# A recommendation kernel on one core: GpSimd takes a product of each of the first two chunks, VectorE reads factors from PSUM

## The chip, the cores and the metric

The kernel runs on one core of one Trainium2 chip. The metric is the device time in microseconds. Before the change it is 501.09 us, the median of three runs (500.9 to 501.11).

Five engines work side by side and meet only at semaphores: TensorE (PE, matmuls out of SBUF into PSUM), VectorE (DVE), ScalarE (ACT), GpSimd (POOL), and SyncE (SP), which here issues nearly all DMAs.

## The reference

A three-layer compressed interaction network for 1024 rows of 64 fields with 16 elements each, everything in float32. Cut to what matters:

```python
x0 = x; h = x; xs = []                                   # x: (1024, 64, 16)
for i in range(3):
    z = jnp.einsum('bfe,bge->bfge', x0, h).reshape(B, 64 * fh, 16)
    y = jnp.einsum('oc,bce->boe', Ws[i], z) + bs[i][None, :, None]   # 128 outputs
    if i != 2:
        x_i, h = y[:, :64], y[:, 64:]                     # half is pooled, half goes on
    else:
        x_i, h = y, y
    xs.append(x_i)
pooled = jnp.sum(jnp.concatenate(xs, axis=1), axis=2)
return pooled @ fc_w.T + fc_b                             # (1024, 1)
```

What is needed is the products of pairs of fields of x (z of the first layer), contracted with weights. As the result is summed and then weighted by `fc_w`, the kernel folds the later layers' weights together beforehand, and contracts the same z with them.

## The kernel before

The 1024 rows are cut into 32 chunks of 32 rows, so that a chunk has N = 512 columns (32 rows by 16 elements). For each chunk two tiles of x are loaded, `xa` (128 partitions, 4 blocks i of 512) and `xb` (4 blocks j of 512). One product per j makes a z tile of 128 x 4 x 512: block i of `xa` times block j of `xb`, so every i meets every j. TensorE then contracts the 16 blocks with the 16 blocks of `w_all`.

```python
HEAD = [4, 5, 6, 0, 1]            # the chunks c0, c1, c2, c3, c4 of the head
NI = NJ = 4

def product(c, j, pieces=1):
    zs[c, j] = z_tile(f"z_{c}_{j}")
    n = NI // pieces
    for i in range(0, NI, n):
        nc.vector.tensor_tensor(
            zs[c, j][:, i : i + n, :], xas[c][:, i : i + n, :],
            xbs[c][j].unsqueeze(1).to_broadcast([128, n, N]), ALU.mult,
        )
    if j == NJ - 1:
        nc.scalar.activation(zs[c, j][SQ, 0, :], xas[c][SQ, 0, :], AF.Square)
```

The head comes first: five chunks are contracted with the first layer's weights only, 64 columns of `w_all` (part 0), while the folded weights (the second 64 columns) are still being made. The first layer's weights of a pair (f, g) and (g, f) are summed on VectorE, one sum for each j; both halves lie in the SBUF tile `w0t`.

```python
def h1_weights(j):
    nc.vector.tensor_tensor(
        w_all[:, j * NI : (j + 1) * NI, 0:64], w0s[j][:, :, 0, :], w0s[j][:, :, 1, :], ALU.add
    )

def half_contract(c, part, j):     # group j of chunk c: 4 blocks, 2 halves of the columns
    cols = slice(part * F, (part + 1) * F)
    rows = slice(0, F) if part == 0 and j == NJ else slice(0, 128)
    for t in (NT,) if j == NJ else range(j * NI, (j + 1) * NI):
        z = zls[c] if t == NT else zs[c, j][:, t % NI, :]
        for n in range(2):
            nc.tensor.matmul(
                accs[c][halves[n]], w_all[rows, t, cols], z[rows, n * H2 : (n + 1) * H2],
                start=(t == 0), stop=(t == NT),
            )
```

In the profile each of these float32 matmuls is two records, so a group is 16 records. `squares(c)` makes the last, smaller tile (`zl`) on ScalarE, and `keep_h1(c)` evacuates a chunk's sums.

The loads in the order of their issue on SyncE (cut to names): first half of xa of c0, block 0 of xb of c0 (`in_xh`), second half of xa of c0, block 0 of w0t (`in_wh`), blocks 1 to 3 of xb of c0, blocks 1 to 3 of w0t, xa and xb of c1, the two 1 MB tiles `w2s`, xa and xb of c2, and `w1s` (1 MB). Then the head of the work:

```python
new_acc(c0, H2)
squares(c0)
for j in range(NJ):
    product(c0, j, 2 if j == 0 else 1)
    if j == NJ - 1:
        nc.vector.memset(w0s[j][SQ, 0, 1, :], 0.0)
    h1_weights(j)
nc.vector.tensor_copy(w_all[0:32, NT, 0:64], w0ds[0:32])
for j in range(NJ + 1):
    half_contract(c0, 0, j)
keep_h1(c0)
squares(c1)
load_chunk(c3)

for n in range(2):                 # sums over w2s with fc weights: pv, evacuated to v2r
    ...
new_acc(c1, H2)
for j in range(NJ - 1):
    product(c1, j)
for j in range(2):
    half_contract(c1, 0, j)
...                                # pt: 32 small matmuls that turn v2r, evacuated to v2t
product(c1, NJ - 1)
half_contract(c1, 0, 2)
load_chunk(c4)

...                                # pm: 8 matmuls of v2t with w1s, evacuated to m_sb on ScalarE
for j in range(3, NJ + 1):
    half_contract(c1, 0, j)
...                                # m_sb goes to DRAM and comes back as folded weights
keep_h1(c1)
...                                # then c2, c3, c4 in the same way, and the other 27 chunks
```

The z tiles turn over 12 buffers, `xa` and `xb` three each. PSUM's eight banks are four of tag `acc` and two each of tags `y` and `set`.

Of the kernel before, what the change touches and what calls it, by code (L numbers as in the profile page):

```python
# [35 lines left out]
F32 = mybir.dt.float32  # L36
# [8 lines left out]
N = CB * E  # L45
NCH = B // CB
NI = 4
NJ = 4
# [8 lines left out]
SQ = slice(96, 128)  # L57
# [3 lines left out]
def cin_kernel(ctx, tc, xra, xrb, xh, wh, w0r, w1h, w2t, wx1, wx0, vec, out):  # L61
    nc = tc.nc
# [6 lines left out]
    ps = ctx.enter_context(tc.tile_pool(name="ps", bufs=2, space=bass.MemoryType.PSUM))  # L69
# [3 lines left out]
    def const_tile(name, shape):  # L73
        return const.tile(shape, F32, tag=name, name=name)

    def z_tile(name):

        return zp.tile([128, NI, N], F32, tag="z", name=name)
# [37 lines left out]
    xas, xbs, zls, xxs = {}, {}, {}, {}  # L116

    def load_xa(c, at=slice(0, NI)):
        if c not in xas or at.start == 0:
            xas[c] = xp.tile([128, NI, N], F32, tag="xa", name=f"xa_{c}")  # L120
        nc.sync.dma_start(
            out=xas[c][:, at, :],
            in_=bass.AP(
                tensor=xra.tensor, offset=c * XR * N + at.start * N,
                ap=[[N, 128], [1, (at.stop - at.start) * N]],
            ),
        )

    def load_chunk(c):
        load_xa(c)  # L130
        xb = xp.tile([128, NJ, N], F32, tag="xb", name=f"xb_{c}")
        nc.sync.dma_start(out=xb, in_=xrb[c])
        xbs[c] = [xb[:, j, :] for j in range(NJ)]

    c0, c1, c2, c3, c4 = HEAD
# [11 lines left out]
    w0s = [w0t[:, j, :].rearrange("p (i v g) -> p i v g", v=2, g=F) for j in range(NJ)]  # L147
# [7 lines left out]
    acc = const_tile("acc", [128, 2, NCH // 2, CB])  # L155
# [3 lines left out]
    def new_acc(c, n=N):  # L159
        accs[c] = ps.tile([128, n], F32, tag="acc", name=f"acc_{c}", bufs=4)  # L160

    def product(c, j, pieces=1):
        zs[c, j] = z_tile(f"z_{c}_{j}")
        n = NI // pieces
        for i in range(0, NI, n):
            nc.vector.tensor_tensor(  # L166
                zs[c, j][:, i : i + n, :], xas[c][:, i : i + n, :],
                xbs[c][j].unsqueeze(1).to_broadcast([128, n, N]), ALU.mult,
            )
        if j == NJ - 1:  # L170
            nc.scalar.activation(zs[c, j][SQ, 0, :], xas[c][SQ, 0, :], AF.Square)  # L171

    def squares(c):
        zls[c] = xp.tile([128, N], F32, tag="zl", name=f"zl_{c}", bufs=4)
        nc.scalar.activation(zls[c][0:64], xas[c][0:64, 0, :], AF.Square)  # L175
# [52 lines left out]
    H2 = N // 2  # L228

    def half_contract(c, part, j):  # L230
# [11 lines that stand above are left out]
    def keep_h1(c):  # L242
        nc.scalar.activation(hb[:, HEAD.index(c), :], accs[c], AF.Identity, bias=bh1)  # L243
# [37 lines left out]
# [4 lines that stand above are left out]
# [1 line left out]

    new_acc(c0, H2)
    squares(c0)
    for j in range(NJ):
        product(c0, j, 2 if j == 0 else 1)  # L290
        if j == NJ - 1:
            nc.vector.memset(w0s[j][SQ, 0, 1, :], 0.0)
        h1_weights(j)
    nc.vector.tensor_copy(w_all[0:32, NT, 0:64], w0ds[0:32])
    for j in range(NJ + 1):
        half_contract(c0, 0, j)
    keep_h1(c0)
    squares(c1)
    load_chunk(c3)


# [2 lines left out]
    for n in range(2):  # L304
# [6 lines left out]
            )  # L311
        nc.scalar.copy(v2r[:, n, :], pv)


    new_acc(c1, H2)
    for j in range(NJ - 1):
        product(c1, j)
    for j in range(2):
        half_contract(c1, 0, j)
    pt = ps.tile([128, F // 4, 4], F32, tag="acc", name="pt", bufs=4)  # L320
    v2q = v2r.rearrange("p n (s o) -> p (n s) o", o=F)
    for q in range(F // 4):
        for to in halves:
            nc.tensor.matmul(pt[to, q, :], v2q[:, q, :], pick, start=True, stop=True)
    nc.scalar.copy(v2t, pt.rearrange("p q k -> p (q k)"))
    product(c1, NJ - 1)
    half_contract(c1, 0, 2)
    load_chunk(c4)

# [304 lines left out]
```

## Time and profile before

The page describes one execution of 499.2 us.

| engine | busy us | share of the span | instructions |
|---|---|---|---|
| TensorE, matmuls | 483.8 | 97% | 1814 |
| VectorE | 381.8 | 76% | 233 |
| ScalarE | 92.5 | 19% | 159 |
| GpSimd | 1.4 | 0% | 14 |

The costliest groups of the page: the contractions of the whole chunks (L198, 864 records of 593 ns, overlapping), VectorE's products (L166, 141 of 2270 ns mean), and the head's contractions (L237, 640 records of 389 ns). In 40 slices of the span TensorE reads 9 tenths in all but the first and the last.

How to read it: busy times of TensorE overlap, as a matmul starts before the one ahead of it has ended. So the distance between starts tells more of its rate than the length of one. What stands in brackets at the end of a line of the timeline is the idle time ahead of it, and the instruction whose semaphore ended that. A wait for several semaphores is put down to the one that came last.

### The profile page before, as it was taken

The numbers are of one execution on the slowest core, as the hardware profiler recorded it, in microseconds if no ns is written. First come the engines' busy times: TensorE is split into PE (matmuls) and PEld (weight loads), VectorE is DVE, ScalarE is ACT, GpSimd is POOL, SyncE is SP. The second block draws the span as 40 slices with busy tenths as digits, with TensorE's granted clock in tenths as the row PEclk, the third lists the DMA queues.
The fourth block names the chain that finished last, engine by engine and source line by source line (L and its number), as shares of the span: only waits on it lengthen the run. The fifth ranks groups of instructions, "written<-read, shape, count | busy, mean of one in ns | idle before, by whom it ended". The sixth has DMA issues, their size and how long they took to land.

```text
span 499.2 us, 4338 instructions
## 1 busy us (share of the span) xinstructions
PE 483.8 (97%) x1814; PEld 222.6 (45%) x1814; DVE 381.8 (76%) x233; ACT 92.5 (19%) x159; POOL 1.4 (0%) x14
## 2 busy tenths in 40 slices
PE   3899999999999999999999999999999999999996
PEld 1455654456444344443444434443444434444432
DVE  4999699988999889898777686776877777770302
ACT  1243033122111121312011121111111121010001
POOL 1000000000000000000000000000000000000000
PEclk9999999999999999999999999999999999999999
DMA  8997895353454443446144442333444430000000
GB/s 327 425 419 226 338 421 208 116 230 129 181 235 175 170 174 162 177 175 256 66 169 169 168 168 113 118 136 138 168 169 168 167 131 39 0 0 0 2 0 0
DMA packets 14787, 82.80 MB, mean 166 GB/s; under 512 B 3788, under 2 KB 4460, under 8 KB 5232
## 3 DMA queue, kind: packets, MB, share of 16 engines
q1 hardware_dynamic: 13644, 81.24, 41.5%
q10 hardware_dynamic: 1124, 1.29, 0.9%
q8 instruction: 14, 0.23, 0.2%
q14 instruction: 5, 0.04, 0.0%
HBM read 80.88 MB, written 1.64 MB: 165 GB/s over the span
## 4 chain that ended last, share of the span: by engine, by line
PE 91%; DMA 5%; ACT 1%; ACTq 0%; SPq 0%; DVE 0%; issue 0%
PE acc L198 75%; PE acc L237 11%; DMA w1s<-in_w1h 4%; PE acc L219 2%; DMA xb<-in_xrb 1%; PE acc L211 1%; PE y L267 1%; PE acc L205 1%; PE pm L336 0%; PE po L489 0%; ACT zl L175 0%; ACT zl L181 0%; ACT m_sb L341 0%; ACT xx L190 0%; ACTq L360 0%
## 5 line engine op out<-in xcount | busy, mean ns | idle before, releaser
L198 PE MATMUL acc<-z,w_all 128*128 128x512 f32 x864 | 374.1, 593 | 0.0
L166 DVE TENSOR_TENSOR z<-xa,xb 128x2048 f32<-128x2048 f32 (+1 forms) x141 | 314.9, 2270 | 49.9 <-PE acc L198 39.7
L198 PEld LDWEIGHTS acc<-z,w_all 128*128 128x128 f32 x864 | 163.3, 190 | 208.3 <-issue 207.8
L237 PE MATMUL acc<-z,w_all 128*64 128x256 f32 x640 | 74.7, 389 | 10.4 <-DVE w_all L282 8.4
L171 ACT ACTIVATE z<-xa 32x512 f32<-32x512 f32 x35 | 21.9, 625 | 323.5 <-DVE z L166 320.7
L263 DVE SCALAR_TENSOR_TENSOR uu<-acc,vs,q 64x512 f32<-64x512 f32 x27 | 20.2, 750 | 62.4 <-ACT q L262 62.3
L237 PEld LDWEIGHTS acc<-z,w_all 128*64 128x64 f32 x640 | 45.8, 140 | 39.1 <-DVE w_all L282 9.9
L274 DVE TENSOR_REDUCE acc<-uu 128x64 f32<-128x1024 f32 (+2 forms) x18 | 20.2, 1125 | 0.3
L190 ACT COPY xx<-xa 64x512 f32<-64x512 f32 x32 | 19.6, 613 | 0.4
L262 ACT COPY q<-acc 64x512 f32<-64x512 f32 x27 | 15.7, 580 | 19.3 <-PE y L224 12.9
L186 ACT ACTIVATE sq<-xa 32x512 f32<-32x512 f32 x24 | 15.1, 628 | 0.6
L270 DVE SCALAR_TENSOR_TENSOR uu<-y,cx,xx 128x512 f32<-128x512 f32 x16 | 11.4, 745 | 0.3
L224 PE MATMUL y<-xx,bd 64*64 64x512 f32 x48 | 11.6, 602 | 0.0
L219 PE MATMUL acc<-xx,v1w 64*64 64x512 f32 x48 | 11.6, 602 | 0.0
L211 PE MATMUL acc<-sq,w_sq 32*128 32x512 f32 x48 | 6.8, 640 | 0.0
L175 ACT ACTIVATE zl<-xa 64x512 f32<-64x512 f32 x11 | 6.8, 623 | 0.1
L219 PEld LDWEIGHTS acc<-xx,v1w 64*64 64x64 f32 x48 | 2.8, 132 | 7.9 <-issue 7.9
L237 PE MATMUL acc<-zl,w_all 64*64 64x256 f32 (+1 forms) x40 | 6.1, 393 | 0.0
L243 ACT ACTIVATE hb<-acc,vs 128x256 f32<-128x256 f32 x5 | 2.4, 474 | 20.0 <-PE acc L237 20.0
L495 ACT ACTIVATE res<-po,cst 2x480 f32<-2x480 f32 (+1 forms) x2 | 0.9, 464 | 24.0 <-PE po L489 24.0
L181 ACT COPY zl<-xa 64x512 f32<-64x512 f32 x8 | 4.9, 616 | 0.1
L256 DVE TENSOR_TENSOR uu<-acc,hb 64x256 f32<-64x256 f32 x10 | 4.2, 421 | 0.2
(52 smaller groups left out, 52.0 us busy)
## 6 DMA issues: line engine op xcount, KB each, us to landing
xa<-in_xra SPq DMA_DIRECT2D x34, 1024.0 KB, 4.8
xb<-in_xrb SPq DMA_DIRECT2D x34, 1024.0 KB, 7.0
w<-in_w2t SPq DMA_DIRECT2D x2, 1024.0 KB, 13.5
xa<-in_xra SPq DMA_DIRECT2D x2, 512.0 KB, 4.1
w1s<-in_w1h SPq DMA_DIRECT2D x1, 1024.0 KB, 20.3
w1x<-in_wx SPq DMA_DIRECT2D x1, 1024.0 KB, 8.7
w0x<-in_wx SPq DMA_DIRECT2D x1, 1024.0 KB, 10.3
xb<-in_xrb SPq DMA_DIRECT2D x1, 768.0 KB, 7.0
```

The lines of the kernel that those rows point to most:

```text
L166: nc.vector.tensor_tensor(zs[c, j][:, i : i + n, :], xas[c][:, i : i + n, :], xbs[c][j].unsqueeze(1).to_broadcast([128, n, N]), ALU.mult,)
L171: nc.scalar.activation(zs[c, j][SQ, 0, :], xas[c][SQ, 0, :], AF.Square)
L186: nc.scalar.activation(zls[c // 4][at : at + 32], xas[c][0:32, 0, :], AF.Square)
L190: nc.scalar.copy(xxs[c // 2][to], xas[c][to, 0, :])
L198: nc.tensor.matmul(accs[c], w_all[:, t, w_cols(c)], zs[c, j][:, i, :], start=(t == 0 and (c < FIRST or c % 4 < 2)), stop=(t == NT - 1 and ...
L211: nc.tensor.matmul(accs[c], w_sq[at, w_cols(c)], zls[first // 4][at], start=(r >= 2), stop=(r < 2), tile_position=(32 * r, 0),)
L219: nc.tensor.matmul(accs[c][q], v1w[rows], xxs[k][rows], start=False, stop=(c % 4 < 2), skip_group_check=True,)
L224: nc.tensor.matmul(ys[k][rows], bd[rows, rows], xxs[k][rows], start=True, stop=True)
L237: nc.tensor.matmul(accs[c][halves[n]], w_all[rows, t, cols], z[rows, n * H2 : (n + 1) * H2], start=(t == 0), stop=(t == NT),)
L262: nc.scalar.copy(q[h], accs[c][64 - h.start : 128 - h.start])
L263: nc.vector.scalar_tensor_tensor(uu, accs[c][h], bh1[h], q[h], ALU.add, ALU.mult)
L274: nc.vector.tensor_reduce(acc[rows, parts, k, :], uus[k][rows, parts].rearrange("p k (b e) -> p k b e", e=E), AX.X, ALU.add,)
```

## The change

GpSimd, which has nothing to do after its first memsets, makes the last product (j = 3) of chunks c0 and c1. ScalarE copies the second factors of c0 (j = 1, 2) and of c1 (j = 0, 1, 2) into free PSUM banks, and VectorE reads them there: its other products of these chunks then have only one input in SBUF, which is meant to keep it out of the way of GpSimd's reads. The last weight sum of W0 (j = 3) does not wait for a product of VectorE any more and comes earlier, and group 0 of c1 is contracted ahead of the sums over w2s instead of behind them. No product, sum or matmul is left out; five ScalarE copies are added.

```diff
-    def product(c, j, pieces=1):
+    def to_psum(c, j, tag):
+
+        t = ps.tile([128, N], F32, tag=tag, name=f"xp_{c}_{j}", bufs=4 if tag == "acc" else 2)
+        nc.scalar.copy(t, xbs[c][j])
+        xbs[c][j] = t
+
+    def product(c, j, pieces=1, engine=nc.vector):
         zs[c, j] = z_tile(f"z_{c}_{j}")
         n = NI // pieces
         for i in range(0, NI, n):
-            nc.vector.tensor_tensor(
+            engine.tensor_tensor(
                 zs[c, j][:, i : i + n, :], xas[c][:, i : i + n, :],
                 xbs[c][j].unsqueeze(1).to_broadcast([128, n, N]), ALU.mult,
             )
@@
     squares(c0)
-    for j in range(NJ):
-        product(c0, j, 2 if j == 0 else 1)
-        if j == NJ - 1:
-            nc.vector.memset(w0s[j][SQ, 0, 1, :], 0.0)
+    product(c0, 0, 2)
+    h1_weights(0)
+    for j in (1, 2):
+        to_psum(c0, j, "y")
+    product(c0, 3, engine=nc.gpsimd)
+    for j in (1, 2):
+        product(c0, j)
         h1_weights(j)
+    nc.vector.memset(w0s[3][SQ, 0, 1, :], 0.0)
+    h1_weights(3)
     nc.vector.tensor_copy(w_all[0:32, NT, 0:64], w0ds[0:32])
     for j in range(NJ + 1):
         half_contract(c0, 0, j)
+
+
+    for j, tag in enumerate(("acc", "acc", "y")):
+        to_psum(c1, j, tag)
     keep_h1(c0)
     squares(c1)
+    product(c1, 3, engine=nc.gpsimd)
+    for j in range(3):
+        product(c1, j)
+    new_acc(c1, H2)
+    half_contract(c1, 0, 0)
     load_chunk(c3)
@@ (after the sums over w2s)
-
-    new_acc(c1, H2)
-    for j in range(NJ - 1):
-        product(c1, j)
-    for j in range(2):
-        half_contract(c1, 0, j)
+    half_contract(c1, 0, 1)
+
+
     pt = ps.tile([128, F // 4, 4], F32, tag="acc", name="pt", bufs=4)
@@
     nc.scalar.copy(v2t, pt.rearrange("p q k -> p (q k)"))
-    product(c1, NJ - 1)
     half_contract(c1, 0, 2)
     load_chunk(c4)
```

## The prediction

> **What bounds the kernel now.** I read the page's shares first, then the waits of TensorE at the head, then the timelines of TensorE and VectorE there.
>
> ```profile
> PE 483.8 (97%) x1814; PEld 222.6 (45%) x1814; DVE 381.8 (76%) x233; ACT 92.5 (19%) x159; POOL 1.4 (0%) x14
> PE 91%; DMA 5%; ACT 1%; ACTq 0%; SPq 0%; DVE 0%; issue 0%
> ```
>
> TensorE is busy for 97% of the span and is 91% of the chain that ended last. No matmul is taken away, so time can only come out of TensorE's idle gaps. The change touches chunks c0 and c1, so the waits of TensorE in the first 45 us (engine and line, what it waited for, total, times, longest):
>
> ```profile
> PE acc L237 <- DVE w_all L282: 8.4, 1, 8.4
> PE acc L237 <- DVE w_all L294: 1.0, 1, 1.0
> PE acc L237 <- ACT z L171: 0.8, 1, 0.8
> PE pm L336 <- DMA w1s<-in_w1h: 0.3, 1, 0.3
> PE pv L307 <- DMA w<-in_w2t: 0.2, 1, 0.2
> ```
>
> The first, 8.4 us, is the start: input, first product, first weight sum. The change leaves it alone. The rest is small. Where it lies, on TensorE's timeline (start, length, what, idle before it):
>
> ```profile
> 8.44 8.30 PE L237 MATMUL acc<-z,w_all 128*64 128x256 f32 x48 [8.44 <-DVE w_all L282]
> 17.73 1.95 PE L237 MATMUL acc<-z,w_all 128*64 128x256 f32 x16 [0.99 <-DVE w_all L294]
> ...
> 30.00 1.95 PE L336 MATMUL pm<-w1s,v2t 64*64 64x512 f32 x16 [0.30 <-DMA w1s<-in_w1h]
> ...
> 40.50 1.95 PE L237 MATMUL acc<-z,w_all 128*64 128x256 f32 x16 [0.77 <-ACT z L171]
> ```
>
> The 48 matmul records of c0's groups j=0,1,2 take 8.30 us here, and 5.40 us later for 48 of the same shape. Part of that is clock: by a table of busy stretches the first 16 records fill 8.44 to 11.9 (3.46 us, 0.216 each); later 48 in 5.40 are 0.112 each. The fourth group waits to 17.73, behind this VectorE chain:
>
> ```profile
> 9.58 2.29 DVE L166 TENSOR_TENSOR z<-xa,xb 128x2048 f32<-128x2048 f32 x1 [1.19 <-DMA xb<-in_xrb]
> 11.79 0.42 DVE L282 TENSOR_TENSOR w_all<-w0t 128x256 f32<-128x256 f32 x1
> 12.12 2.28 DVE L166 TENSOR_TENSOR z<-xa,xb 128x2048 f32<-128x2048 f32 x1
> 14.32 0.42 DVE L282 TENSOR_TENSOR w_all<-w0t 128x256 f32<-128x256 f32 x1
> 14.66 2.29 DVE L166 TENSOR_TENSOR z<-xa,xb 128x2048 f32<-128x2048 f32 x1
> 17.01 0.11 DVE L292 MEMSET w0t<- 32x64 f32 x1
> 17.16 0.42 DVE L282 TENSOR_TENSOR w_all<-w0t 128x256 f32<-128x256 f32 x1
> 17.50 0.17 DVE L294 COPY w_all<-vs 32x64 f32<-32x64 f32 x1
> ```
>
> So VectorE paces c0, and the change takes one 2.29 us product out of this chain. But the pm matmuls at 30.00 wait for the 1 MB of w1s, issued at 9.57 and 20.3 us to landing, that is 29.87. Nothing in the change moves that transfer, and before it the queue is full (the DMA view of the first 36 us has some 400 to 460 GB/s in its slices once started). What TensorE wins before 30.0 turns into a longer wait for w1s.
>
> **What the Trainium skill says.** "SBUF — State Buffer", section "Who interferes with whom": a VectorE instruction with two SBUF inputs contends with a GpSimd instruction that reads SBUF, one with at most one SBUF input does not, and whichever issues first has the shared ports for its whole instruction. This is what the PSUM copies are for. The trace before cannot confirm it: GpSimd does 1.4 us of memsets there. "GPSIMD Engine Reference", section 3.1: a 2048-element fp32 tensor_tensor takes 4497 ns on GpSimd and 2293 ns on VectorE. The trace agrees on VectorE (2.28 to 2.29); the other has no counterpart. "VectorE: DVE Perf Modes", section "The perf-mode tier table": fp32 tensor_tensor runs at one element per cycle with or without PSUM. The trace agrees: 421 ns with a PSUM input for 256 elements (L256), 0.42 without. "TensorE: Matmul & The Clock Gate", section "What's actually happening": the array runs at half clock until it was busy for some 3.4 us, and falls back after an idle window of that length. The two rates above agree, though the page's granted clock reads full throughout.
>
> **The change, part by part.**
>
> *ScalarE copies.* xb of c0 lands at 9.57 (2.59 plus 6.96). A 128x512 ScalarE copy is 0.58 us (L312), so factor j=1 is in PSUM at 10.2 and j=2 at 10.8. VectorE starts its second product 0.65 us later than now.
>
> *GpSimd's products.* c0's j=3 goes from 9.6 to 14.1 (4.5 us, an estimate from the page named above). The second needs xb of c1, issued at 5.07 and 11.3 to landing, so 16.4: it runs from 16.4 to 20.9.
>
> *VectorE, the part I think decides.* The products with PSUM factors have one SBUF input and should not contend. But h1_weights(1), (2) and (3) add two halves of w0t, both in SBUF, and between the products they meet GpSimd's reads. If the rule holds:
> - product 1: 10.2 to 12.55
> - h1_weights(1): ready at 12.55, held until GpSimd's first product ends, 14.1 to 14.5
> - product 2: 14.5 to 16.8
> - h1_weights(2): ready at 16.8, GpSimd's second product holds the ports since 16.4, so 20.9 to 21.3
> - memset and h1_weights(3): to 21.8
>
> TensorE then starts group 1 at 14.6 instead of 12.26, group 2 at 21.35 instead of 14.8. Groups 2 and 3 at the late rate (1.8 each) and the last small group (0.58) end at 25.5; at present c0 ends at 20.19. That is 5.3 us lost. The slack ahead of pm gives back the waits for w2 and w1s (0.36 and 0.47 beyond the usual distance of starts, some 0.8), leaving 4.5. The idle stretches, 11.9 to 14.6 and about 17 to 21.35, are long enough to keep the array at half clock for one more group or two: each cold group costs 3.4 instead of 1.8, so 1.6 to 3.2 more, though up to 1.6 of it falls in a stretch that is idle anyway. I take 0 to 2.5.
>
> *Moving group 0 of c1 ahead of pv.* It fills the wait for w2 when there is no loss. Same work, other order: 0 to 0.3 us, before 30.0, so hidden.
>
> *c1's offload.* VectorE would be through c1's products 2.3 us sooner in the best case, but its next product needs xb of c2, which lands at 26.4, and that product starts at some 26.6 now (17.60 and four of 2.27). Nothing is gained. The wait of 0.77 at 40.50 hangs on ScalarE's queue after the pm evacuations and stays.
>
> Sum with the rule in force: 501.1 + 4.5 + (0 to 2.5) = 505.6 to 508.1. After 41 us TensorE has no gap left that could absorb it.
>
> **Rivals.**
>
> *No block on the short sums.* h1_weights(1) ends at 13.0, product 2 at 15.3, h1_weights(2) at 15.7, h1_weights(3) at 16.2. Group 2 starts at 15.7, group 3 behind it at 17.5, GpSimd's z and ScalarE's square being ready at 14.8; c0 ends at 19.9 against 20.19. c1's group 0 waits for nothing (xb at 16.4, three copies, product by 19.5), pm is ready at about 29.2 and waits for w1s. Time: 500.4 to 501.4, the same but for w1s landing some tenths earlier or later. For it speaks that somebody who put factors into PSUM knew of the contention; against it, the sums were left in SBUF in the middle of it.
>
> *GpSimd slower than the estimate.* Its first product also waits behind an extra library instruction on its queue. If that shows up as a few microseconds at the first product, it ends at 16 to 20, and group 3 or the held sums come later still: 503.5 without the block, 508 to 511 with it. Nothing in this trace has GpSimd reading tensors, so I can't exclude it.
>
> *A real gain.* It needs w1s to land sooner. Its last packets fall behind the bulk, since 1 MB at 420 GB/s is 2.5 us and w1s follows xb of c2 (issued at 7.48, 18.9 to landing, 26.4) by 3.5. If that lag went away, up to 0.9 us would come out: 500.2.
>
> **Range and chances.** I give the block 0.6, and within it 505.6 to 508.1 with a tail to 511 for a slow GpSimd; no block 0.3, at 500.4 to 501.4; between, 0.1. Two humps, so the middle is a compromise at the lower edge of the larger one: 505.6. The range 500.5 to 509.5 covers both humps without the slow tail. Faster by 2% would be 491.1, a gain of 10 us where TensorE's gaps beyond the start add up to some 5 (8.30 less 5.40, and the four short waits): 0.01. Slower by 2% is 511.1, only the slow tail: 0.07. Within 2%: 0.92.
>
> **What would show it.** In the changed profile: GpSimd's two products, near 9.6 and 16.4, about 4.5 us each. VectorE's h1_weights(1) and (2) starting, or lasting, to the ends of GpSimd's products (near 14.1 and 20.9) shows the block; at 12.6 and 15.3 with 0.42 each it refutes it. Products with PSUM factors at 2.3 us beside GpSimd show that they do not contend; 4 us or more would mean they do, and a worse loss. c0's last matmul near 25.5 against 19.9, and pm's start at 34.5 or later against 30.0, are the sizes. The prediction is wrong if pm starts at 30.0 whatever happens before, or if time is lost after 41 us.

## The result and the profile after

The changed kernel takes 508.07 us (median of 4 runs, 507.56 to 508.44) against 501.08: a ratio of 1.0139, 95% interval 1.0124 to 1.0154. It is slower by 7 us. The profiled execution, the fastest of the four, spans 505.8 us against 499.2, which is 6.5 us more; the other three are 0.4 to 0.9 us slower. In the page's 40 slices TensorE's row begins with 2 and 5, where the row before begins with 3 and 8 (so it does not read 9 in all but the first and the last slice: the second one, from 12.5 to 25 us, was short already).

TensorE's waits over the whole span (engine and line, what it waited for, total, times, longest), changed kernel:

```profile
PE acc L243 <- DVE w_all L288: 14.6, 3, 8.7
PE po L505 <- DVE acc L280: 2.0, 1, 2.0
PE acc L243 <- ACT z L177: 0.9, 1, 0.9
```

The wait for the weight sums (L288, `h1_weights`) has grown from one of 8.4 us to three of 14.6. The waits for w2, for w1s and for c0's last copy are gone: TensorE comes too late to meet them. VectorE's timeline says why (start, length, what, idle before it):

```profile
10.19 2.29 DVE L172 TENSOR_TENSOR z<-xa,xp 128x2048 f32<-128x2048 f32 x1 [1.56 <-ACT xp L165]
12.40 2.12 DVE L288 TENSOR_TENSOR w_all<-w0t 128x256 f32<-128x256 f32 x1
14.45 2.27 DVE L172 TENSOR_TENSOR z<-xa,xp 128x2048 f32<-128x2048 f32 x1
16.64 4.63 DVE L288 TENSOR_TENSOR w_all<-w0t 128x256 f32<-128x256 f32 x1
21.34 0.11 DVE L303 MEMSET w0t<- 32x64 f32 x1
21.49 0.43 DVE L288 TENSOR_TENSOR w_all<-w0t 128x256 f32<-128x256 f32 x1
```

And GpSimd's two products beside them:

```profile
9.71 4.53 POOL L172 TENSOR_TENSOR z<-xa,xb 128x2048 f32<-128x2048 f32 x1 [7.43 <-DMA xb<-in_xrb]
16.48 4.51 POOL L172 TENSOR_TENSOR z<-xa,xb 128x2048 f32<-128x2048 f32 x1 [2.24 <-DMA xb<-in_xrb]
```

Read the two together. The products with a factor in PSUM (`xp`) run at 2.27 to 2.29 us beside GpSimd's: no contention. The sums of 256 elements take 0.43 us when GpSimd is idle, but the one at 12.40 ends at 14.52 and GpSimd's first product at 14.24; the one at 16.64 ends at 21.27 and the second product at 20.99. Each was held to some 0.3 us behind the end of GpSimd's instruction. The hold is inside the record's length: VectorE counts as busy in it, so its idle times do not show it. The engines thus do not meet only at semaphores: VectorE and GpSimd also get in each other's way at SBUF, and e1 shows that it depends on where VectorE reads.

TensorE's timeline follows:

```profile
8.69 3.28 PE L243 MATMUL acc<-z,w_all 128*64 128x256 f32 x16 [8.69 <-DVE w_all L288]
14.58 3.46 PE L243 MATMUL acc<-z,w_all 128*64 128x256 f32 x16 [2.61 <-DVE w_all L288]
21.33 5.36 PE L243 MATMUL acc<-z,w_all 128*64 128x256 f32 x32 [3.29 <-DVE w_all L288]
...
27.20 1.95 PE L243 MATMUL acc<-z,w_all 128*64 128x256 f32 x16
...
36.40 1.95 PE L352 MATMUL pm<-w1s,v2t 64*64 64x512 f32 x16
...
46.99 1.95 PE L243 MATMUL acc<-z,w_all 128*64 128x256 f32 x16 [0.85 <-ACT z L177]
```

Group 1 of c0 starts at 14.58 (12.26 before), group 2 at 21.33 (14.80 before), pm at 36.40 (30.00), c2's last group at 46.99 (40.50), which is 6.49 later. TensorE's last matmul is also 6.49 later: after 47 us nothing is lost or won. Group 1 takes 3.46 us where 1.95 is usual, and groups 2 and 3 together 5.36 where 3.67 is. Here is the granted clock, in stretches (from:to, length, busy time and records of PE and of its loads, PEclk, DMA share, GB/s), of line L243:

```profile
11.50:14.80 3.30, 0.69 (x8) 0.21 (x6) 1.00 1.01 427
14.90:18.20 3.30, 3.13 (x16) 1.36 (x12) 0.50 1.01 427
18.30:21.60 3.30, 0.27 (x3) 0.20 (x5) 1.00 1.02 427
21.70:25.00 3.30, 3.30 (x20) 1.84 (x18) 0.50 1.01 422
25.10:27.00 1.90, 1.90 (x20) 0.96 (x16) 1.00 1.03 427
```

The clock is full where the array stands idle and half where it has work: each step follows how busy the array was in the stretch before it (0.69 us of 3.30, then 0.50; 3.13, then 1.00; 0.27, then 0.50; 3.30, then 1.00). Only the second held sum is paid twice, though. Group 1's slow run ends at 18.04, in a time in which group 2 waits for its weights until 21.33 anyway. What the half clock costs is the 1.69 us of groups 2 and 3.

The clock's reading has a gap at the start. It is 1.00 from 8.5 to 11.4 us too, but group 0's 16 records take 3.28 us there, the slow rate. The trace's first clock record comes at 11.4 us (13.3 in the kernel before); ahead of it only the lengths tell the rate.

### The profile page after: what moved, and what is told of

Same layout as the page of the kernel before. It is cut to its first block, busy times and chain, and to the rows that moved or that the text cites. A ratio compares the mean times of both kernels' runs of the same rounds, so it can differ in the third digit from the quotient of the medians.

```text
span 505.8 us, 4346 instructions
## 1 busy us (share of the span) xinstructions
PE 485.8 (96%) x1814; PEld 223.5 (44%) x1814; DVE 383.3 (76%) x231; ACT 95.5 (19%) x164; POOL 10.4 (2%) x16
## 4 chain that ended last, share of the span: by engine, by line
PE 93%; DVE 2%; ACT 2%; DMA 1%; ACTq 0%; SPq 0%; issue 0%
PE acc L204 74%; PE acc L243 13%; PE acc L225 2%; DMA xb<-in_xrb 1%; DVE w_all L288 1%; PE acc L217 1%; DVE z L172 1%; PE y L273 1%; PE acc L211 1%; PE po L505 0%; PE pm L352 0%; PE pv L327 0%; PE pt L341 0%; ACT zl L181 0%; ACT zl L187 0%; ACTq L376 0%
## 5 line engine op out<-in xcount | busy, mean ns | idle before, releaser
L172 DVE TENSOR_TENSOR z<-xa,xb 128x2048 f32<-128x2048 f32 (+1 forms) x134 | 299.4, 2269 | 50.7 <-PE acc L204 41.8
L243 PE MATMUL acc<-z,w_all 128*64 128x256 f32 x640 | 77.0, 398 | 15.4 <-DVE w_all L288 14.6
L243 PEld LDWEIGHTS acc<-z,w_all 128*64 128x64 f32 x640 | 46.7, 143 | 45.5 <-DVE w_all L288 15.9
L268 ACT COPY q<-acc 64x512 f32<-64x512 f32 x27 | 15.7, 580 | 19.3 <-PE y L230 12.9
L172 DVE TENSOR_TENSOR z<-xa,xp 128x2048 f32<-128x2048 f32 x5 | 11.2, 2273 | 1.6 <-ACT xp L165 1.6
L276 DVE SCALAR_TENSOR_TENSOR uu<-y,cx,xx 128x512 f32<-128x512 f32 x16 | 11.4, 746 | 0.3
L172 POOL TENSOR_TENSOR z<-xa,xb 128x2048 f32<-128x2048 f32 x2 | 9.0, 4518 | 9.7 <-DMA xb<-in_xrb 9.7
L288 DVE TENSOR_TENSOR w_all<-w0t 128x256 f32<-128x256 f32 x4 | 7.6, 1900 | 0.0
L243 PE MATMUL acc<-zl,w_all 64*64 64x256 f32 (+1 forms) x40 | 6.1, 393 | 0.0
## 6 DMA issues: line engine op xcount, KB each, us to landing
w1s<-in_w1h SPq DMA_DIRECT2D x1, 1024.0 KB, 19.3
```

Source lines behind the costliest of these rows:

```text
L172: engine.tensor_tensor(zs[c, j][:, i : i + n, :], xas[c][:, i : i + n, :], xbs[c][j].unsqueeze(1).to_broadcast([128, n, N]), ALU.mult,)
L243: nc.tensor.matmul(accs[c][halves[n]], w_all[rows, t, cols], z[rows, n * H2 : (n + 1) * H2], start=(t == 0), stop=(t == NT),)
L268: nc.scalar.copy(q[h], accs[c][64 - h.start : 128 - h.start])
L288: nc.vector.tensor_tensor(w_all[:, j * NI : (j + 1) * NI, 0:64], w0s[j][:, :, 0, :], w0s[j][:, :, 1, :], ALU.add)
```

## The experiments

My theory: the sums with both inputs in SBUF are held by GpSimd's products, the half clock adds to it, and the rest of the change neither harms nor helps because the loads limit the head. The rivals: GpSimd's products cost by themselves; the sums are slow for another reason; the reordering costs.

**e1: the first sum reads one half from PSUM.** One ScalarE copy is added, into a bank of tag `set` that is free there.

```diff
+    def weights_to_psum(j):
+        t = ps.tile([128, NI * F], F32, tag="set", name=f"wp_{j}")
+        wp[j] = t.rearrange("p (i g) -> p i g", g=F)
+        nc.scalar.copy(wp[j], w0s[j][:, :, 1, :])
     ...
-            w_all[:, j * NI : (j + 1) * NI, 0:64], w0s[j][:, :, 0, :], w0s[j][:, :, 1, :], ALU.add
+            w_all[:, j * NI : (j + 1) * NI, 0:64], w0s[j][:, :, 0, :],
+            wp[j] if j in wp else w0s[j][:, :, 1, :], ALU.add
     ...
+    weights_to_psum(1)
     product(c0, 3, engine=nc.gpsimd)
```

> The changed kernel, plus one ScalarE copy of the second half of w0t's j=1 into PSUM, so that h1_weights(1) has one SBUF input; nothing else differs. Port theory: that sum takes 0.42 us instead of 2.12 and ends near 13.0; product 2 ends near 15.2, so h1_weights(2), still with both inputs in SBUF, falls into GpSimd's pause between its products (14.2 to 16.5) and takes 0.42 instead of 4.63; pm starts near 30.0 and the time is 500.4 to 501.4 us. Rival, GpSimd's products cost TensorE time by themselves or the sums are slow for another reason (strides, the load of w0t): h1_weights(2) stays at 4 us or more and the time near 508.

Measured: 502.38 us (ratio 1.0025, 1.0014 to 1.0035). VectorE's timeline of e1:

```profile
12.56 0.41 DVE L295 TENSOR_TENSOR w_all<-w0t,wp 128x256 f32<-128x256 f32 x1
...
15.09 0.42 DVE L295 TENSOR_TENSOR w_all<-w0t 128x256 f32<-128x256 f32 x1
```

Moving one operand of one 0.42 us instruction gives back 5.7 of the 7 us. The second sum, still with both inputs in SBUF, falls into GpSimd's pause and is free as well, so nothing in the sums themselves makes them slow. The half clock goes too: TensorE's waits shrink to 0.48 and 0.34 us, and groups 2 and 3 take 3.67. GpSimd's products are unchanged (4.55 and 4.58 us), so the first rival falls. The time is 1 us above what I expected, and TensorE's timeline of e1 shows where:

```profile
30.68 1.95 PE L361 MATMUL pm<-w1s,v2t 64*64 64x512 f32 x16 [1.66 <-DMA w1s<-in_w1h]
...
49.63 1.95 PE L243 MATMUL acc<-z,w_all 128*64 128x256 f32 x16 [0.71 <-ACT z L177]
```

w1s came 0.7 us later than before, and there is a new wait at c3's last group. Both are followed up below.

**e2: only c0's product on GpSimd.**

```diff
-    product(c1, 3, engine=nc.gpsimd)
-    for j in range(3):
+    for j in range(NJ):
         product(c1, j)
```

> The changed kernel, but the last product of c1 back on VectorE; c0's stays on GpSimd. Port theory: h1_weights(1) is still held to 14.5 us, h1_weights(2) runs at 16.7 with 0.42; c0's last group ends near 22.3 instead of 27.2, pm starts near 31.3, and the time is 501.8 to 503.2 us: the second product carries two thirds or more of the loss. Rival, the loss is that of c0's product on GpSimd alone: the time stays within 1 us of 508.

Measured: 504.70 us (ratio 1.0071, 1.0056 to 1.0086). The first sum is held as in the change (12.53, 2.12 us), the second is not (16.77, 0.41 us). c0's last group ends at 22.2, as expected, and pm starts at 31.78. TensorE's timeline of e2:

```profile
42.40 1.95 PE L243 MATMUL acc<-z,w_all 128*64 128x256 f32 x16 [0.88 <-ACT z L177]
...
51.55 1.95 PE L243 MATMUL acc<-z,w_all 128*64 128x256 f32 x16 [1.29 <-ACT z L177]
```

By c2's last group (40.50 before) 1.90 us are lost, then another 1.5 at c3's, where ScalarE's square is late. The time is 1.5 us above the expected range. About half of the change's 7 us goes with the second product (3.4 us); it would be 70%, an estimate, without the loss at c3, which the expectation did not have.

**e3: no PSUM copies.** The two loops over `to_psum` are taken out.

> The changed kernel without the five ScalarE copies: VectorE's products of c0 and c1 read both factors from SBUF, beside GpSimd's products. Port theory with turns taken in order of arrival: the products and the sums are held up to 4.5 us each, group 2 of c0 starts at 24 us or later, 508.5 to 511 us. If VectorE's queue keeps the ports instead until it runs dry: GpSimd's first product is held to about 15.5, z of j=3 comes late, 502 to 504 us. Rival, no contention of products with GpSimd: VectorE's products run at 2.3 us each and the time is that of the change, 508, or a little less.

Measured: 509.77 us (ratio 1.0174, 1.0159 to 1.0189), 1.7 above the change and in the range of the first expectation (group 2 starts at 23.22, a little before 24). GpSimd's timeline of e3, then VectorE's:

```profile
9.54 6.50 POOL L172 TENSOR_TENSOR z<-xa,xb 128x2048 f32<-128x2048 f32 x1 [7.26 <-DMA xb<-in_xrb]
16.30 6.58 POOL L172 TENSOR_TENSOR z<-xa,xb 128x2048 f32<-128x2048 f32 x1 [0.26 <-DMA xb<-in_xrb]
```

```profile
9.39 2.29 DVE L172 TENSOR_TENSOR z<-xa,xb 128x2048 f32<-128x2048 f32 x1 [0.98 <-DMA xb<-in_xrb]
11.61 4.72 DVE L288 TENSOR_TENSOR w_all<-w0t 128x256 f32<-128x256 f32 x1
```

They take turns in the order of arrival, as far as these two pairs show it. VectorE's product came first (9.39), so GpSimd's record stretches from 4.5 to 6.50; then the sum waits for GpSimd, although VectorE's queue had it ready. The copies of the change do what they are for; they were only not made for the sums.

**e4: dummy matmuls in TensorE's idle stretches**, 11 behind group 0 and 16 behind group 1, into a tile nobody reads.

```diff
     for j in range(NJ + 1):
         half_contract(c0, 0, j)
+        for _ in range({0: 11, 1: 16}.get(j, 0)):
+            nc.tensor.matmul(dm[halves[0]], w_all[:, 0, 0:64], zs[c0, 0][:, 0, 0:H2], start=True, stop=True)
```

> The changed kernel with 27 extra matmuls of c0's shape into a PSUM tile that nothing reads, 11 behind group 0 and 16 behind group 1, to keep TensorE active where it waits for VectorE. If 1.6 us or so of the loss is the array at half clock after the idle stretches, groups 1 to 3 run at 1.8 us each, c0 ends near 25.6 instead of 27.2 and the time is 506.0 to 506.9 us. If the slow groups are due to something else (GpSimd's reads, DMA), they stay slow and the time is 508 or more.

Measured: 511.79 us (ratio 1.0211, 1.0194 to 1.0228). A fault of the experiment: all dummies write one column half, and they take twice as long as intended (behind group 1, 31 records take 6.85 us; in e8, where they alternate between the halves, 32 take 3.62). They ran from 12.06 to 18 and from 19.8 to 26.5 and put off the real groups. It says nothing of the clock's cost; e8 mends it.

**e5: the reordering alone**, without GpSimd and without copies.

> Only the reordering of the change: no GpSimd product and no PSUM copies; VectorE makes all products from SBUF, c0's last sum follows its last product, and group 0 of c1 is contracted ahead of pv. Theory: the reordering itself costs nothing at the head (c0 ends at 20.2 us, pm starts at w1s's landing, 29.9). But its loads of the folded weights on ScalarE's queue now wait for the semaphores of earlier loads, as in the run with c0 alone on GpSimd, where the square of c3 behind them came 1.5 us late: 501.5 to 502.6 us. Rival, that gap came from c3's data or from the later start alone: 500.6 to 501.3 us.

Measured: 506.18 us (504.41 to 507.32; ratio 1.0103, 1.0087 to 1.0118): outside both expectations. I had put c1's last product, now on VectorE, where the change has it on GpSimd, ahead of pv. With it came its square on ScalarE, which stood there until VectorE was through (26.42) with the evacuations of pv behind it. TensorE's timeline of e5:

```profile
27.70 2.03 PE L336 MATMUL pt<-pick,v2r 128*64 128x4 f32 x64 [1.94 <-ACT v2r L327]
```

That is 1.8 us at pt (25.93 before). In the profiled execution (4.1 us above the profile before) a half-clock stretch then falls on c1's group 2 and on pm (2.82 and 2.68 us, 1.93 and 1.95 at the full rate), and c3's last group waits for its square as in e2. The times scatter with the granted clock, from 504.41 us at 1.000 to 507.32 at 0.992. So e5 does not tell what the reordering costs. e9 does.

**e6: the small loads of the folded weights go to SyncE.** In e1 and e2 ScalarE's queue has two such loads ahead of c3's square, and in e2 both, in e1 the second waits for the semaphore of an earlier load: the issue records name eight DMA semaphores in turn, and moving other instructions moves which load waits for which. In the kernel before neither of the two waits. e6 is e1 with

```diff
-            queue = nc.scalar if half and i < 2 else nc.sync
+            queue = nc.sync
```

> The kernel with the sum from PSUM, and in addition the two small loads of the folded weights that were on ScalarE's queue go to SyncE's. Theory: ScalarE's square of c3 no longer stands behind a load that waits, the gap of 1.1 us before c3's last group goes, and the time falls by 0.7 to 1.0 us, to 501.3 to 501.7; pm still starts with w1s near 30.5. Rival, the gap is due to c3's data or VectorE: no change, 502.4.

Measured: 500.90 us (ratio 0.9998, 0.9990 to 1.0006), the time of the kernel before. TensorE runs through c3 without a gap:

```profile
43.28 7.13 PE L243 MATMUL acc<-z,w_all 128*64 128x256 f32 x64
```

The time came out 0.4 us better than expected, although w1s is still late (pm at 30.48).

**e7: w1s ahead of c2's loads**, on top of e6.

```diff
-    load_chunk(c2)
     nc.sync.dma_start(out=w1s, in_=w1h)
+    load_chunk(c2)
```

> As the kernel with the sum from PSUM and the loads on SyncE, and w1s is issued ahead of the loads of c2. Theory: w1s lands 5 us sooner, so pm starts behind c1's group 2 at 28.9 to 29.3 instead of 30.7; c2's data land later, at 28 to 30.5, so that VectorE's products of c2 set the next limit: c2's last group near 40.4 instead of 41.06, and the time is 500.3 to 501.2 us. Rival, w1s is not what holds TensorE there: no change against the kernel with the loads on SyncE.

Measured: 501.42 us (ratio 1.0015, 1.0008 to 1.0022). pm starts at 28.87, 1.6 us sooner than in e6. At c2's last group, which now waits longer, 0.7 us of it is left (40.82 in e6):

```profile
40.13 1.95 PE L243 MATMUL acc<-z,w_all 128*64 128x256 f32 x16 [1.46 <-ACT z L177]
```

At c3's last group (a wait of 0.40) the rest goes, and TensorE's last matmul starts within 0.04 us of e6's. The wait for w1s did stand at pm, but behind it stands the next transfer, c2's xb: it lands at 29.85, against 27.84 in e6, and VectorE's first product of c2 follows at 29.97 (27.97). The time is 0.5 us above e6 and 0.2 above the expected range; 5 of the 20 runs took 503.0 to 503.2 us, and the trace, of a run of 501.32, does not show why.

**e8: the dummies mended**: 6 and 16, alternating between the column halves, and the loads on SyncE. It has the change's two held sums (4.6 us for the second, group 2 at 21.26).

```diff
+        for k in range({0: 6, 1: 16}.get(j, 0)):
+            nc.tensor.matmul(
+                dm[halves[k % 2]], w_all[:, 0, 0:64], zs[c0, 0][:, 0, 0:H2], start=True, stop=True
+            )
```

> The changed kernel with dummy matmuls again, but fewer and shared between the two column halves as the real groups are: 6 behind group 0 and 16 behind group 1 of c0; the two small loads of the folded weights are on SyncE's queue. Theory (1.6 us or so of the loss is the half clock after the idle stretches): the clock stays full from about 14 us on, groups 2 and 3 run at 1.8 us each from 21.4, c0's last group ends near 25.6 instead of 27.2 and the time is 506.0 to 507.0 us. Rival: no change in the rate of groups 2 and 3, 507.6 to 508.4 us.

Measured: 506.00 us (ratio 1.0099, 1.0085 to 1.0112). TensorE's timeline of e8:

```profile
12.06 2.68 PE L310 MATMUL dm<-z,w_all 128*64 128x256 f32 x12
14.57 1.89 PE L243 MATMUL acc<-z,w_all 128*64 128x256 f32 x16
16.30 3.62 PE L310 MATMUL dm<-z,w_all 128*64 128x256 f32 x32
21.26 3.67 PE L243 MATMUL acc<-z,w_all 128*64 128x256 f32 x32 [1.34 <-DVE w_all L288]
24.87 0.65 PE L243 MATMUL acc<-zl,w_all 64*64 64x256 f32 x4
25.45 1.95 PE L243 MATMUL acc<-z,w_all 128*64 128x256 f32 x16
```

The first dummies still run at the slow rate (0.22 us a record), all that follows at the full one (0.11), and the granted clock reads 1.00 up to 25 us. Groups 2 and 3 take 3.67 us instead of 5.36; c1 begins at 25.45 instead of 27.20. So some 1.75 us of the change's loss is the half clock. The moved loads have no part in it: pm (34.65), c2's last group (45.24) and TensorE's last matmul are sooner by the same 1.75. By the medians 22 matmuls that compute nothing make the kernel 2 us faster.

**e9: the reordering alone, mended**, with c1's last product behind pt and the loads on SyncE.

> The reordering alone again, without GpSimd's products and without PSUM copies, but with c1's last product where it was before (behind pt), so that ScalarE's square of it does not stand ahead of the evacuations of pv as it did in the last run; the two small loads of the folded weights are on SyncE's queue. Theory: group 0 of c1 ahead of pv costs and brings nothing, because pm waits for w1s at 29.9 to 30.3 in any order: 500.7 to 501.4 us. Rival, the reordering has a cost of its own: 502 us or more.

Measured: 500.90 us (ratio 0.9999, 0.9991 to 1.0008). With the two loads on SyncE the reordering is neutral. It was not run alone with the loads where the change has them, but the changed kernel's trace shows no wait at c3.

**e10 and e11: ScalarE's squares for c3 and c4 behind c2's last square**, in e6 and in the kernel before.

```diff
     squares(c2)
-    for c in KEPT:
-        last_tile(c)
-    def head(c):
+    def head(c, also=()):
         new_acc(c, H2)
         for j in range(NJ):
             product(c, j)
+        for n in also:
+            last_tile(n)
     ...
-    head(c2)
+    head(c2, KEPT)
```

> The kernel with the sum from PSUM and the loads on SyncE, and six ScalarE operations for c3 and c4 (their squares and copies, 3.7 us) moved behind the square of c2's last z tile. Theory: c2's last group no longer waits 0.8 us for that square; what is gained there lies behind the wait for w1s and so stays: 499.9 to 500.3 us, faster than both kernels. Rival, VectorE's product for that group is late too (c2's data land at 28): half or less of the gain, 500.5 to 500.9 us.

Measured: 500.03 us (ratio 0.9983, 0.9976 to 0.9989). TensorE's wait for c2's last z is gone, and c2 runs through (e10, then e11):

```profile
34.30 7.13 PE L243 MATMUL acc<-z,w_all 128*64 128x256 f32 x64
```

```profile
34.55 7.13 PE L237 MATMUL acc<-z,w_all 128*64 128x256 f32 x64
```

> The kernel before with nothing but the same move of six ScalarE operations. Theory: the same 0.6 to 0.8 us, 500.2 to 500.5 us; so that with and without GpSimd's products the time is the same within 0.3 us, and the offload has no worth of its own even where it does no harm. Rival, the offload relieves VectorE for c2: this kernel gains at least 0.3 us less than the one with GpSimd.

Measured: 500.02 us (ratio 0.9984, 0.9977 to 0.9990). Both are faster than the kernel before by 0.9 us, and the same within 0.01; e11 is 0.2 below its expected range. With its harm mended and the next wait removed, the offload to GpSimd still brings nothing that the kernel before does not reach with VectorE alone.

## Why the prediction was right, and where it was loose

The step "VectorE, the part I think decides" held within 0.2 us: first sum to 14.5 (measured 14.52), second held from 16.8 to 21.3 (16.64 to 21.27), group 1 at 14.6 (14.58), group 2 at 21.35 (21.33). GpSimd's 4.5 us, then an estimate from the Trainium skill's "GPSIMD Engine Reference", section 3.1, measured 4.53 and 4.51. The rule of its "SBUF — State Buffer", section "Who interferes with whom", that the sum was made with agrees with the change, e1 and e3: with two inputs in SBUF VectorE's sum takes 2.12 us beside GpSimd, with one 0.41.

The sum, term by term, at c2's last group in the profiled executions. In the kernel before, c0 ends where pv begins:

```profile
20.19 1.07 PE L307 MATMUL pv<-w,fv 128*32 128x512 f32 x8
```


| term | predicted us | measured us | from |
|---|---|---|---|
| c0 ends later, sums held | 5.3 | 5.26 | e8: 25.45 against 20.19 |
| half clock | 0 to 2.5 | 1.75 | 27.20 against 25.45 |
| slack ahead of pm | -0.8 | -0.61 | pm 6.40 later, c0's end 7.01 later |
| after pm, to 47 us | 0 | 0.09 | 6.49 less 6.40 |
| sum | 4.5 to 7.0 | 6.49 | |

The slack is smaller than predicted because the wait for w1s was worth 0.37 us, not 0.47, and group 0 of c1 ahead of pv costs 0.14: it makes one block of 32 records into two of 16.

"TensorE: Matmul & The Clock Gate", section "What's actually happening", gave the right length of window: each half-clock stretch of the change lasts 3.41 us in the clock's records. As the prediction put it, the clock falls back after an idle window of that length; here it did so after less, an idle stretch of 2.61 us at 11.97 and one of 3.29 at 18.04. That the page's clock before reads full throughout was no evidence against a slow start, as its first record comes at 13.3 us only.

The point of 505.6 was too low by 2.5 us. The mechanism was right and the sum under it (505.6 to 508.1) just holds the result; the 0.5 us between the profile's 6.49 and the medians' 7.0 is not explained. What was off is the point. I gave the rule 0.6 and took a middle that lay at that hump's lower edge, which leaves nothing for the half clock. That the result lies in the range says little, as the range was wide enough for the opposite mechanism too; what speaks for the mechanism is the times of the two sums. There was little reason for 0.3 on "no block": it rested on what the change's author may have known, not on the trace.

The rivals. "No block on the short sums" fell at once, but its time is what e6 and e9 show when the sums are not held (500.9, predicted 500.4 to 501.4). "GpSimd slower than the estimate" fell: its first product starts 0.14 us behind its data, so whatever the library instruction ahead of it costs is hidden in the 7.43 us in which GpSimd waits for that data. "A real gain" needs w1s sooner: w1s did land sooner in the change (19.3 us after issue against 20.3), and TensorE was too late to use it. e7 shows that w1s sooner by issue order buys nothing, because c2's xb comes later for it.

The step "nothing is gained" for c1's offload is supported by e10 against e11. The step that pm's wait for w1s absorbs what is won before it held, but I had taken w1s's landing as fixed, and it moved by 1.7 us between kernels (below).

## What to carry to other kernels

Before an elementwise product moves to GpSimd, list every VectorE instruction that can run beside it with two SBUF inputs, the short ones too: two sums of 0.42 us took 2.1 and 4.6. One operand of the first in PSUM freed both, the second because it then fell between GpSimd's products. Look at what the relieved engine waits for next: here the loads set the pace of the first 40 us, so relieving VectorE could not pay. When moving instructions around, look at each in-order queue for what is now behind the moved one (e5), and at which loads now wait for which semaphore (e1, e2).

## What the runs showed of the hardware beyond that

The landing of w1s, from the view of that tile (before, change, e1 in this order):

```profile
DMA to landing us min/median/max: 20.3/20.3/20.3
```

```profile
DMA to landing us min/median/max: 19.3/19.3/19.3
```

```profile
DMA to landing us min/median/max: 20.8/20.8/20.8
```

From issue at 9.57, 9.56 and 9.73 that is 29.87, 28.85 and 30.54. Between 20 and 33 us each of these traces has one 16 KB packet of instructions on a queue of its own, of 1.07 to 1.10 us, beginning at 26.0, 31.0 and 23.3. I take it for TensorE's: in every trace 190 to 242 of TensorE's records, weight loads included, begin before it. In the ten traces in which it comes ahead of w1s's end, with the loads in this order, the last of the sixteen parts of w1s lands 0.9 to 1.7 us behind the fifteenth, at 29.8 to 30.5. Where it comes later (the change, and e3 with 32.5), the last part is less than 0.1 us behind, and w1s lands at 28.85 and 28.66. A faster TensorE reaches that point of its instructions sooner, so that a faster head would delay its own weights. This is an inference from traces that agree; no run moved the fetch by itself.

A held instruction's wait is counted as busy time (2.12 and 4.63 us for a 0.43 us sum; 6.50 for a 4.5 us product on GpSimd). Such a hold appears in no list of waits: only an instruction of odd length beside others of its form gives it away.
